# Selected rows of a routed layer processed one batch at a time

## The chip, the core and the metric

The kernel runs on one core of a Trainium2 chip. A core has five engines that work side by side, each through its own instructions in order: TensorE (PE, matrix products and transposes), VectorE (DVE), ScalarE (ACT), GpSimd (POOL) and SyncE (SP, which here only issues DMA transfers). They meet through semaphores. The metric is the time of one execution on the device, in microseconds (us); less is better.

## The reference

Two sequences (batches) of 2048 rows of 512 numbers go through four parts, each added to the rows with a gate:

```python
x = x + tanh(g_xattn[0]) * L0_xattn(layernorm(x), ctx)   # 16 heads over 128 context rows
x = x + tanh(g_ffn[0])   * L0_ffn(layernorm(x))          # routed, see below
x = x + tanh(g_xattn[1]) * L1_xattn(layernorm(x), ctx)   # 16 heads of 64
x = x + tanh(g_ffn[1])   * L1_ffn(layernorm(x))          # ternary weights, a convolution
```

The second part is the one that the change concerns. It sends only 256 of the 2048 rows of each batch through a small layer, and leaves the others as they are:

```python
_, idx = top_k(x @ w_router, 256)
x_sel = x[idx]                                # per batch
h = rmsnorm(x_sel, g1)
q, k, v = split(h @ W_qkv.T)                  # 16 heads of 32
o = softmax(causal(q @ k.T / sqrt(32))) @ v
x_attn = o @ W_out.T
h2 = rmsnorm(x_sel + x_attn, g2)
x_ff = silu(h2 @ W1.T) * (h2 @ W2.T) @ W3.T   # 1365 hidden columns
out = x.at[idx].set(x_sel + x_attn + x_ff)
```

Nothing in it mixes the two batches.

## The kernel before

A row tile is 128 rows of 512 numbers; a block is four row tiles (512 rows), so there are eight blocks, four for each batch. The stages follow each other in the program text; a scheduler then orders the instructions of each engine, mostly by their place in the text and by when their inputs and buffers are ready, and adds the semaphore waits.

**First cross attention, with the router beside it.** `cross_attention` runs 16 units per block (`U`), each one head: scores (L271), softmax (L116 to L128), transposes (L289), values (L297). `front` normalizes and transposes a block's rows, `back` multiplies with the output weights (L315) and updates the residual rows `x` (L324). All 32 row tiles of `x` stay in SBUF from the start (`load_x`, L430). When a block's rows are done, `router` (L442) is appended to `pending`; its steps are taken by `beside`, two after every unit. A router step normalizes rows again, writes them to `xn_d`, scores them (L462), writes the scaled residual to `x_d` (L473), and then counts on DVE for every row how many rows of its batch score higher (`count`, L492, and L514 for the 128 rows of the own tile). After the last block of a batch, `gather` makes one-hot matrices of the ranks (L537), multiplies them into the row numbers `idx` (L541, L555), and POOL fetches the 256 chosen rows into `xs` with an indirect DMA (L557). The router of the very last block has no units left to stand beside: it is drained by the loop at L589.

**Selected attention.** Both batches' 512 chosen rows are treated as one block (L644 to L785). `rms_block` normalizes and transposes them (L626), L674 makes values, `queries_keys` (L692) queries and keys of four heads at a time for both batches, 512 columns wide. `selected_probabilities` takes one batch: scores (L711), mask and maximum on DVE (L721, L722), exponentials on ACT (L727), a product with the reciprocal on POOL (L737). `selected_values` transposes (L747), copies (L748) and multiplies with the values (L752); it is called one step behind, so that one batch's softmax stands beside the other's products. L775 is the output projection; a second `rms_block` makes `h2T`.

**Feed-forward.** 1365 hidden columns in 11 chunks of 128 (`NF`). A chunk loads three slices of weights (`load_ffn`, three chunks ahead), multiplies two of them with `h2T`, 512 columns wide (L875), applies Silu (L883) and a product (L885), and accumulates the third (L861) into four PSUM tiles. Beside it, `quantized_weights` reads the two weight matrices of the last part, sums their absolute values (L819), and makes them ternary (L836 on ACT, L841 and L842 on DVE). At the end POOL adds the result into `x_d` with an indirect DMA (L902), four times.

**Second cross attention.** `W1.keys_values()` (L912) makes keys (L182) and values (L200) of the context; then `cross_attention` runs again, with rows from `x_d` (`xf`, L1143), residual rows read a second time, a bias added to them on POOL (L311), and the last part beside it.

Of the kernel before, what the change touches and what calls it, by code (L numbers as in the profile page):

```python
# [17 lines left out]
P = 128  # L18
# [3 lines left out]
BLK = 512  # L22
# [21 lines left out]
def flamingo_kernel(ctx: ExitStack, tc: tile.TileContext, a: dict, out: bass.AP):  # L44
# [91 lines left out]
    class CrossWeights:  # L136
# [38 lines left out]
        def keys_values(self):  # L175
            L, nE, bias = self.L, self.nE, self.bias
            with ExitStack() as st:
                ps0 = psum_pool(st, L + "ps0", 2)
                for e in range(nE):
                    pk = ps0.tile([P, B * M], F32, name="pk", tag="pk")  # L180
                    for c in range(CC):
                        nc.tensor.matmul(  # L182
                            pk,
                            self.wk[:, c, ts(e, P)],
                            self.ctxT[:, c, :],
                            start=(c == 0),
                            stop=(c == CC - 1),
                        )
                    src = pk.rearrange("p (b m) -> p b m", b=B)
                    if bias:  # L190
                        nc.vector.tensor_scalar(
                            self.kT[:, :, e, :], src, self.bk[:, e : e + 1], None, ALU.add
                        )
                    else:
                        nc.vector.tensor_copy(self.kT[:, :, e, :], src)
                for b in range(B):
                    for n in range(nE * P // 512):
                        pv = ps0.tile([P, 512], F32, name="pv", tag="pv")
                        for c in range(CC):
                            nc.tensor.matmul(  # L200
                                pv,
                                self.ctxT[:, c, ts(b, M)],
                                self.wv[:, c, ts(n, 512)],
                                start=(c == 0),
                                stop=(c == CC - 1),
                            )
                        to = self.v[:, b, ts(n, 512)]
                        if bias:
                            nc.vector.tensor_tensor(to, pv, self.bv[:, ts(n, 512)], ALU.add)
                        else:  # L210
                            nc.scalar.copy(to, pv)
# [159 lines left out]
    sel_stack = ExitStack()  # L371
# [19 lines left out]

    with ExitStack() as st:
        xres = st.enter_context(tc.tile_pool(name="xres", bufs=1))
        x = [xres.tile([P, D], F32, name=f"x{i}") for i in range(NT)]
        rp = st.enter_context(tc.tile_pool(name="router", bufs=1))
# [34 lines left out]
        def load_x(i):  # L430
            for t in range(i * TB, (i + 1) * TB):
                nc.sync.dma_start(out=x[t], in_=x_in[t])

        pending = []
# [7 lines left out]
        def router(n, tiles):  # L442
# [13 lines left out]
            for i in range(TB):  # L456
                t = t0 + i
                xn = act.tile([P, D], F32, name="xn2", tag="xn2", bufs=2)
                normalize(xn, x[t], mv, rstd, i)
                nc.sync.dma_start(out=xn_d[b][ts(t - b * TPB, P), :], in_=xn)  # L460
                ws = act.tile([P, D], F32, name="ws2", tag="ws2", bufs=1)
# [21 lines left out]
        def ranks(b, blk):  # L483
# [6 lines left out]
            def count(t, lo, hi, op, k):  # L490
                junk = rp.tile([P, S], BF16, name="junk", tag="junk", bufs=2)
                nc.vector.tensor_scalar(  # L492
                    junk[:, lo:hi], sb[b][:, lo:hi], own(t), None, op, ALU.add,
                    accum_out=cnt[b][:, t, k : k + 1],
                )
# [71 lines left out]
        with ExitStack() as st0:  # L567
            W0.load_context(st0, "left")
            load_x(0)
            W0.load_rest()  # L570
            for i in range(1, B * NBLK):
                load_x(i)
            W0.keys_values()
        act = st.enter_context(tc.tile_pool(name="L0_act", bufs=2))
        row = st.enter_context(tc.tile_pool(name="L0_row", bufs=8))
        ps_mm = psum_pool(st, "L0_mm", 2)
        ps_sc = psum_pool(st, "L0_sc", 4)
        ps_o = psum_pool(st, "L0_o", 2)

        def stage1_rows(n):  # L580
            tiles = x[n * TB : (n + 1) * TB]
# [7 lines left out]
        while pending:  # L589
            beside(None)  # L590


    right, right1, right2 = ExitStack(), ExitStack(), ExitStack()
# [3 lines left out]
    with ExitStack() as st:  # L597
        AHEAD = 3
        wst = st.enter_context(tc.tile_pool(name="wst", bufs=AHEAD))
        keepp = st.enter_context(tc.tile_pool(name="keepp", bufs=1))  # L600
        w13 = {}

        def load_ffn(f):
            n = min(P, DFF - f * P)
            w1c = wst.tile([P, DC, P], F32, name="w1c", tag="w1c")
            nc.sync.dma_start(
                out=w1c[:, :, :n], in_=row_tiles(a["W1T"])[:, :, ds(f * P, n)]
            )
            w2c = wst.tile([P, DC, P], F32, name="w2c", tag="w2c")
            nc.sync.dma_start(  # L610
                out=w2c[:, :, :n], in_=row_tiles(a["W2T"])[:, :, ds(f * P, n)]
            )
            w3c = wst.tile([P, D], F32, name="w3c", tag="w3c")
            nc.sync.dma_start(out=w3c[:n, :], in_=a["W3T"][ds(f * P, n), :])
            w13[f] = (w1c, w2c, w3c)

        g1 = keepp.tile([P, DC], F32, name="g1")
        nc.sync.dma_start(out=g1, in_=a["g1"])
        g2 = keepp.tile([P, DC], F32, name="g2")
        nc.sync.dma_start(out=g2, in_=a["g2"])  # L620
        xa = [keepp.tile([P, D], F32, name=f"xa{i}") for i in range(4)]

        def wide(name):
            return keepp.tile([P, DC, BLK], F32, name=name, tag="wide", bufs=2)

        def rms_block(tiles, gcol, dst, pool, ps, tag, name):  # L626

            ss = pool.tile([P, 4], F32, name=name + "_ss", tag="rms_ss")
            hn = [pool.tile([P, D], F32, name="hn", tag="hn", bufs=4) for _ in tiles]
            for i, t in enumerate(tiles):  # L630
                nc.scalar.activation(hn[i], t, AF.Square, accum_out=ss[:, i : i + 1])
            r = rsqrt(4, ss, 1.0 / D, 1e-6, small, name + "_r")
            for i, t in enumerate(tiles):
                nc.vector.tensor_scalar(hn[i], t, r[:, i : i + 1], None, ALU.mult)
            transpose_block(
                ps,
                tag,
                hn,
                lambda d, pt: nc.vector.tensor_scalar(
                    dst[:, d, :], pt, gcol[:, d : d + 1], None, ALU.mult  # L640
                ),
            )

        with ExitStack() as sa:  # L644
            w = sa.enter_context(tc.tile_pool(name="w_attn", bufs=1))
            act = sa.enter_context(tc.tile_pool(name="act_attn", bufs=1))
            row = sa.enter_context(tc.tile_pool(name="row_attn", bufs=6))
            ps_mm = psum_pool(sa, "s2_mm", 2)
            ps_sc = psum_pool(sa, "s2_sc", 4)
            ps_tp = psum_pool(sa, "s2_tp", 2)  # L650

            wqkv = w.tile([P, DC, 3 * D], F32, name="wqkv")
            for n in range(3):
                nc.sync.dma_start(
                    out=wqkv[:, :, ts(n, D)], in_=row_tiles(a["WqkvT"])[:, :, ts(n, D)]
                )
            wout = w.tile([P, DC, D], F32, name="wout")
            nc.sync.dma_start(out=wout, in_=row_tiles(a["WoutT"]))
            for f in range(AHEAD):
                load_ffn(f)  # L660

            mask = w.tile([P, 3, P], F32, name="mask")
            nc.gpsimd.memset(mask[:, 1, :], 0.0)
            for k in (0, 2):
                make_causal_mask(nc, mask[:, k, :], NEG)

            hT = wide("hT")
            rms_block(xs, g1, hT, act, ps_tp, "tp", "rms1")

            v2 = act.tile([P, 4, D], F32, name="v2")  # L670
            for i in range(4):
                pv = ps_mm.tile([P, D], F32, name="pv2", tag="mm")
                for d in range(DC):
                    nc.tensor.matmul(  # L674
                        pv,
                        hT[:, d, ts(i, P)],
                        wqkv[:, d, ds(2 * D, D)],
# [3 lines left out]
                nc.scalar.copy(v2[:, i, :], pv)  # L681

            OT = wide("OT2")

            def queries_keys(c):

                qc = act.tile([P, BLK], F32, name="qc", tag="qc", bufs=2)
                kc = act.tile([P, BLK], F32, name="kc", tag="kc", bufs=2)
                pq, pk = [ps_mm.tile([P, BLK], F32, name=n, tag="mm") for n in ("pq2", "pk2")]
# [73 lines left out]
            for c in range(DC):  # L763
                qc, kc = queries_keys(c)
                for b in range(B):
                    A = selected_probabilities(qc, kc, b)
                    if behind:
                        selected_values(*behind)
# [590 lines left out]
```

## Time and profile before

| | us |
|---|---|
| median of five runs | 1854.13 (1853.56 to 1855.94) |
| the profiled execution | 1853.55 |
| its span, first to last instruction | 1851.8 |
| PE busy in the span | 1658.2 (90%) |
| DVE busy | 1311.9 (71%) |
| ACT busy | 1051.4 (57%) |
| POOL busy | 526.5 (28%) |

The page gives busy time of each engine, the same in 40 slices of the span, the chain of work that ended last, and groups of equal instructions with their mean duration and the idle time ahead of them. An engine's busy share is a mean over stages; what one stage costs is read from its own stretch. The granted clock of PE is a share of its full speed; its mean here is 0.952. The first cross attention ends at 531.6 us of the span, the second begins at 835.0.

### The profile page before, as it was taken

Reading aid. Unit: us, or ns where it says so; the run is one execution under the profiler, and the core shown is the slowest. Engines: PE = TensorE matmul, PEld = TensorE weight load, DVE = VectorE, ACT = ScalarE, POOL = GpSimd, SP = SyncE. Lnnn points to the kernel's source line nnn. Section 1 sums busy time; section 2 is a strip of 40 time slices with the busy share of each in tenths; the row PEclk is TensorE's granted clock in tenths of the full one; section 3 lists DMA queues with packets and bytes.
Section 4 is the critical chain, followed back from the end, with each engine's and each line's share of the span. In section 5 each row is a group of like instructions: output and inputs, shape, how many; then the busy total and the mean of one; then the engine's idle time right before and its main releaser. Section 6 shows DMA issues by size and latency. Waiting matters only on the chain.

```text
span 1851.8 us, 24500 instructions
## 1 busy us (share of the span) xinstructions
PE 1658.2 (90%) x7706; PEld 832.6 (45%) x7706; DVE 1311.9 (71%) x2769; ACT 1051.4 (57%) x3065; POOL 526.5 (28%) x666
## 2 busy tenths in 40 slices
PE   6989988888836989989999999999999999898969
PEld 3544544444413444445544454444444454443423
DVE  5777898787783642224537789889888888876966
ACT  2645545354501536304537778878787787754556
POOL 4534434342300320032214233332423243220200
PEclk9999999899967889999999999999999999998989
DMA  7011011011144009330011233334134133255465
GB/s 287 1 46 47 1 47 46 12 46 47 46 141 154 1 11 313 111 91 23 29 37 50 97 114 105 128 118 155 52 130 129 73 116 120 77 203 202 152 226 194
DMA packets 98456, 184.36 MB, mean 100 GB/s; under 512 B 11327, under 2 KB 30527, under 8 KB 94614
## 3 DMA queue, kind: packets, MB, share of 16 engines
q1 hardware_dynamic: 97430, 180.70, 28.1%
q0 software_dynamic: 896, 2.10, 0.6%
q8 instruction: 61, 1.00, 0.2%
q14 instruction: 69, 0.57, 0.1%
HBM read 108.31 MB, written 74.45 MB: 99 GB/s over the span
## 4 chain that ended last, share of the span: by engine, by line
PE 38%; DVE 13%; DMA 5%; ACT 4%; POOL 2%; issue 2%; SPq 1%; POOLq 0%; DVEq 0%; ACTq 0%
PE pp L315 9%; PE pq L248 8%; PE ph L1002 3%; DVE h L1018 3%; PE sc L271 3%; PE po L297 2%; PE pu L875 2%; PE tp L289 2%; PE acc L861 2%; PE pw L875 2%; PE po L1231 2%; DMA hq<-hq_d 1%; DMA x<-h_d 1%; DVE u L1012 1%; DVE AT L290 1%
## 5 line engine op out<-in xcount | busy, mean ns | idle before, releaser
L119 ACT ACTIVATE A<-sc,nmx 128x128 f32<-128x128 f32 x1024 | 362.8, 376 | 174.4 <-DVE nmx L116 152.1
L128 POOL TENSOR_TENSOR A<-A,rden 128x512 f32<-128x512 f32 x256 | 274.7, 1074 | 479.6 <-DVE rden L127 368.4
L315 PE MATMUL pp<-L_wo,OT 128*128 128x512 f32 x768 | 365.9, 610 | 13.8 <-DVE x L324 4.7
L248 PE MATMUL pq<-xnT,L_wq 128*128 128x512 f32 x768 | 355.6, 609 | 0.0
L119 ACT ACTIVATION_READ_ACCUMULATOR A<-sc,nmx 128x1 f32 x1024 | 220.7, 216 | 0.0
L116 DVE TENSOR_REDUCE nmx<-sc 128x4 f32<-128x512 f32 x256 | 169.3, 678 | 66.4 <-PE sc L271 66.4
L248 PEld LDWEIGHTS pq<-xnT,L_wq 128*128 128x128 f32 x768 | 144.9, 196 | 158.5 <-issue 150.9
L290 DVE COPY AT<-tp 128x512 f32<-128x512 f32 x256 | 173.2, 678 | 56.0 <-PE tp L289 55.5
L315 PEld LDWEIGHTS pp<-L_wo,OT 128*128 128x128 f32 x768 | 138.7, 195 | 160.4 <-issue 134.3
L1018 DVE SCALAR_TENSOR_TENSOR h<-u,cw,h 128x512 f32<-128x512 f32 x256 | 191.6, 784 | 5.8 <-ACT h L1014 5.4
L289 PE MATMUL tp<-ident,A 128*128 128x128 f32 x1024 | 164.1, 282 | 30.0 <-POOL A L128 28.4
L271 PE MATMUL sc<-L_kT,qT 32*128 32x128 f32 (+1 forms) x2048 | 164.7, 292 | 6.6 <-ACT A L119 4.9
L271 PEld LDWEIGHTS sc<-L_kT,qT 32*128 32x128 f32 (+1 forms) x2048 | 131.2, 190 | 85.9 <-issue 59.7
L289 PEld LDWEIGHTS tp<-ident,A 128*128 128x128 f32 x1024 | 119.3, 143 | 105.1 <-issue 47.6
L1231 PE MATMUL po<-w2q,hq 128*128 128x512 bf16 x512 | 120.6, 391 | 18.1 <-DVE hq L1213 8.5
L1014 ACT ACTIVATE h<-u,cb,cw 128x512 f32<-128x512 f32 x128 | 99.1, 809 | 64.6 <-DVE u L1012 59.9
L1002 PE MATMUL ph<-xiT,w1q 128*128 128x512 bf16 x512 | 125.2, 381 | 2.6 <-DVE u L1012 2.4
L297 PE MATMUL po<-AT,L_v 128*32 128x512 f32 (+1 forms) x512 | 116.0, 625 | 8.0 <-DVE AT L290 7.6
L305 ACT COPY OT<-po 128x512 f32<-128x512 f32 x96 | 55.7, 588 | 101.2 <-PE po L297 100.8
L1012 DVE TENSOR_TENSOR u<-ph,inv_b 128x512 f32<-128x512 f32 x128 | 85.2, 684 | 31.0 <-PE ph L1002 26.1
L1011 POOL COPY u<-carry 128x2 f32<-128x2 f32 x128 | 49.7, 390 | 193.6 <-DVE h L1018 161.3
L311 POOL TENSOR_TENSOR x<-x,L_bo 128x512 f32<-128x512 f32 x64 | 86.8, 1374 | 34.2 <-DMA x<-x_d 8.2
(216 smaller groups left out, 2203.6 us busy)
## 6 DMA issues: line engine op xcount, KB each, us to landing
h_d<-h SPq DMA_DIRECT2D x28, 1024.0 KB, 3.9
x_d<-x SPq DMA_DIRECT2D x64, 256.0 KB, 2.6
hf<-h_d SPq DMA_DIRECT2D x64, 256.0 KB, 3.2
x<-x_d SPq DMA_DIRECT2D x61, 256.0 KB, 4.2
x<-h_d SPq DMA_DIRECT2D x48, 256.0 KB, 5.5
x<-in_x SPq DMA_DIRECT2D x32, 256.0 KB, 5.4
xn_d<-xn SPq DMA_DIRECT2D x32, 256.0 KB
xf<-x_d SPq DMA_DIRECT2D x32, 256.0 KB, 4.1
```

The lines of the kernel that those rows point to most:

```text
L116: nc.vector.tensor_reduce(nmx, sc, AX.X, ALU.max, negate=True)
L119: nc.scalar.activation(out_tile[:, h, :], sc[:, h, :], AF.Exp, bias=nmx[:, h : h + 1], accum_out=den[:, h : h + 1],)
L128: nc.gpsimd.tensor_tensor(out_tile, out_tile, rden.unsqueeze(2).to_broadcast([P, n, width]), ALU.mult,)
L248: nc.tensor.matmul(pq, W.wq[:, d, ts(e, P)], xnT[:, d, :], start=(d == 0), stop=(d == DC - 1),)
L271: nc.tensor.matmul(sc[h][:, t, :], qT[e % cpg][r, ts(t, P)], W.kT[r, b, e, :], start=True, stop=True,)
L289: nc.tensor.transpose(tp[:, t, :], A[:, t, :], ident)
L290: nc.vector.tensor_copy(AT, tp.rearrange("p t n -> p (t n)"))
L297: nc.tensor.matmul(po[h * dh : (h + 1) * dh, :], W.v[:, b, ts(hd, dh)], AT[c * hpc + h], start=True, stop=True,)
L315: nc.tensor.matmul(pp, OT[e][:, ts(i, P)], W.wo[:, e, :], start=(e == 0), stop=(e == nE - 1),)
L1002: nc.tensor.matmul(ph, w1q[:, d, ts(c, P)], xiT[g][:, d, :], start=(d == 0), stop=(d == DC - 1),)
L1018: nc.vector.scalar_tensor_tensor(z, u[:, ds(k, BLK)], cw[:, c, k : k + 1], z, ALU.mult, ALU.add)
L1231: nc.tensor.matmul(po, rows(c), w2q[:, c, :], start=(c == 0), stop=(c == HC - 1))
```

## The change

The selected rows are no longer one block of 512 but two of 256, each with its own attention and its own feed-forward.

- `selected_attention(b, ...)` is a generator: it yields after every small step. The first batch's is driven after the cross attention, with two calls of `beside` (each up to two router steps) after each of its own steps, and so stands beside the last block's router. The second batch's is handed to the feed-forward of the first, which takes five of its steps after every chunk, and two of the ternary weights' steps.
- `feed_forward(b, ...)` runs twice, 256 columns wide, with two accumulators; each run loads all weights of the layer. Beside the second run stand the keys and values of the next cross attention, of which `keys_values` is now a generator too. Each run scatters its own two row tiles into `x_d`.
- The residual rows are a ring of twelve row tiles: `load_x(n)` is called from `stage1_rows`, and a tile's buffer is free again when its scaled row is written to `x_d`.
- The weights `wqkv` are loaded at the start of the kernel, and `w1q` lies in the pool `const`.
- PSUM: while the feed-forward of the first batch runs, three banks are shared by its products, the queries, keys and values, two serve the scores, one the transposes and the products with the values, two accumulate.

```diff
-        x = [xres.tile([P, D], F32, name=f"x{i}") for i in range(NT)]
+    xres = router_stack.enter_context(tc.tile_pool(name="xres", bufs=3 * TB, side="right"))
...
+        def load_x(n):
+            if n * TB not in x:
+                for t in range(n * TB, (n + 1) * TB):
+                    x[t] = xres.tile([P, D], F32, name="x", tag="x")
+                    nc.sync.dma_start(out=x[t], in_=x_in[t])
...
-                junk = rp.tile([P, S], BF16, name="junk", tag="junk", bufs=2)
+                junk = rp.tile([P, S], BF16, name="junk", tag="junk", bufs=1)
...
-            for i in range(1, B * NBLK):
-                load_x(i)
-            W0.keys_values()
+            for n in (1, 2):
+                load_x(n)
+            for n in range(3):
+                nc.sync.dma_start(
+                    out=wqkv[:, :, ts(n, D)], in_=row_tiles(a["WqkvT"])[:, :, ts(n, D)]
+                )
+            with ExitStack() as st1:
+                for _ in W0.keys_values(psum_pool(st1, "L0_ps0", 2), "kv"):
+                    pass
...
         def stage1_rows(n):
-            tiles = x[n * TB : (n + 1) * TB]
+            load_x(n)
+            tiles = [x[t] for t in range(n * TB, (n + 1) * TB)]
...
-        while pending:
-            beside(None)
...
+    def selected_attention(b, mm, sc_tile, o_tile, together):
+        rows = xs[2 * b : 2 * b + 2]
+        hT = keepp.tile([P, DC, CAP], F32, name="hT", tag="hT", bufs=1)
+        yield from rms_rows(rows, g1, hT, mm)
...
+        qk, behind = (yield from queries_keys(0)), None
+        for c in range(DC):
+            A = yield from probabilities(*qk)
+            if c + 1 < DC:
+                qk = yield from queries_keys(c + 1)
+            if behind:
+                yield from values(*behind)
+            behind = A, c
+        yield from values(*behind)
...
+        yield from rms_rows(rows, g2, h2T[b], mm)
...
+    with ExitStack() as sp:
+        ps_mm = psum_pool(sp, "s2_mm", 2)
+        ps_sc = psum_pool(sp, "s2_sc", 4)
+        first = selected_attention(
+            0, in_pool(ps_mm, "mm"), in_pool(ps_sc, "sc"), in_pool(ps_o, "o"), 4
+        )
+        for _ in first:
+            for _ in range(2):
+                beside(None)
+        while pending:
+            beside(None)
...
+            for f in range(NF):
+                n = min(P, DFF - f * P)
+                pu, pw = mm([P, CAP], "pu"), mm([P, CAP], "pw")
...
+                if f > 0:
+                    down(f - 1)
+                    if f - 1 + AHEAD < NF:
+                        load(f - 1 + AHEAD)
+                after_chunk(f)
+                for w, n in work:
+                    for _ in range(n):
+                        next(w, None)
...
+    with ExitStack() as sp:
+        mm = in_pool(psum_pool(sp, "s2b_mm", 3), "mm")
+        ps_sc = psum_pool(sp, "s2b_sc", 2)
+        ps_tp = psum_pool(sp, "s2b_o", 1)
+        second = selected_attention(1, mm, in_pool(ps_sc, "sc"), in_pool(ps_tp, "o"), 2)
+        feed_forward(
+            0,
+            psum_pool(sp, "s2b_acc", 1),
+            mm,
+            [(lambda st: second, 5), (lambda st: quantized_weights(st, mm), 2)],
+        )
...
+    with ExitStack() as sp:
+        mm = in_pool(psum_pool(sp, "s2c_mm", 3), "mm")
+        ps_kv = psum_pool(sp, "s2c_kv", 3)
+        feed_forward(
+            1,
+            psum_pool(sp, "s2c_acc", 1),
+            mm,
+            [(lambda st: W1.keys_values(ps_kv, "kv"), 2)],
+            lambda f: W1.load_rest() if f == 1 else None,
+        )
...
-    W1.keys_values()
```

The products, the softmax and the ternary weights are computed as before, on half as many columns at a time. Of the selected attention's small operations one is new in count: the minimum of two maxima is taken per head (four on 128x1) and not once for four heads.

## The prediction, made before the changed kernel was run

> **What bounds the kernel now.** I read the page's slices first, to see where TensorE (PE) is not full and its clock falls; then the busy times of four stretches in the middle; then PE and VectorE (DVE) in order of time; last the instruction groups, for durations.
>
> ```profile
> PE   6989988888836989989999999999999999898969
> ...
> PEclk9999999899967889999999999999999999998989
> ```
>
> A slice is 46.3 us. PE is the full engine nearly everywhere; the one deep hole is slice 12 (509 to 556 us), and the clock is lowest around it. The stretches:
>
> ```profile
> core 0: us, PE busy (x) PEld busy (x) DVE busy (x) ACT busy (x) POOL busy (x), PEclk, DMA share, GB/s
> 531.64:575.87 44.23, 5.27 (x37) 2.85 (x37) 31.13 (x96) 6.51 (x13) 5.04 (x9) 0.52 0.81 275
> 575.87:688.83 112.96, 102.52 (x573) 52.31 (x573) 56.04 (x119) 46.87 (x164) 25.35 (x25) 0.91 0.04 14
> 688.83:805.45 116.62, 116.62 (x274) 51.47 (x274) 29.69 (x59) 42.83 (x60) 0.87 (x1) 0.98 0.53 172
> 805.45:835.02 29.57, 20.82 (x74) 13.52 (x72) 9.66 (x24) 2.34 (x4) 16.96 (x18) 0.92 0.59 143
> ```
>
> They are the last block's router, the selected attention of both batches, the feed-forward, and the keys and values of the next cross attention with the wait behind them: 303.4 us from the last residual update (531.64) to the next stage's first transpose (835.02). In the first, PE works 5.3 of 44.2 us while DVE ranks. That hole is what the change aims at.
>
> ```profile
> 521.02 9.83 PE L315 MATMUL pp<-L_wo,OT 128*128 128x512 f32 x16 [4.74 <-DVE x L324]
> ...
> 560.27 4.15 PE L541 MATMUL pi<-place,oh 128*128 128x2 bf16 x32 [20.61 <-DVE oh L537]
> 575.87 1.46 PE L110 MATMUL ptr<-ident,hn 128*128 128x128 f32 x5 [11.45 <-DVE hn L634]
> ```
>
> After 4.74 us of idleness the 16 matmuls of L315 take 9.83 us, where 16 later ones take 6.9: idle PE also loses clock.
>
> **What stays.** From the first transpose of the next stage on, the 4,227 PE instructions stand in the same order in both built programs. So the change is worth what it moves that transpose (835.02) plus what it leaves undone there. PE's arithmetic in the middle is the same too, if 256-wide matmuls cost half of 512-wide ones:
>
> ```profile
> 805.45 10.53 PE L182 MATMUL pk<-L_ctxT,L_wk 128*128 128x256 f32 x48
> 815.81 10.46 PE L200 MATMUL pv<-L_wv,L_ctxT 128*128 128x512 f32 x24
> 835.02 1.34 PE L110 MATMUL ptr<-ident,xf 128*128 128x128 f32 x5 [8.75 <-issue]
> ```
>
> 10.36 us (to the next start) over 48 is 0.216 us, and 10.46 over 24 is 0.43: half, with weight loads hidden (each f32 matmul is two such instructions). Splitting the feed-forward by batch doubles its weight loads and its weight traffic, and costs PE nothing.
>
> **Residual ring and early load: 0.** A block's x loads now wait for the x_d writes three blocks before. On SP's queue the loads of block 3 stand right behind block 0's writes, some 13 units ahead of their use; a unit is 3.8 us (eight blocks in 491 us, 16 units each), so 50 us of other work hide 2.6 us of write and 5.4 us of load. Without that cover five blocks would lose 8 us each. The QKV weights (3.1 MB) now load at the start, where five x blocks (5.2 MB) no longer do.
>
> **A: first batch's attention beside the last router.** The built order puts the first two residual updates of the last block ahead of a 1408-wide count; so the 4.74 us wait and the slow clock after it mostly go. The two together are worth at most 4.7 + 2.9; I take 4.6: the last update at 527.0. From there, on DVE:
> - to the first count: 8.7 us now (540.31), plus 2 x 0.48 and 4 x 0.42 of the new rows' normalizing, plus four value matmul pairs that stand on PE ahead of the last score broadcast (4 x 0.86, 4.6 at a partly halved clock): 15.9.
> - to the index: 24.7 now (540.31 to 565.05), plus one chunk's four heads, each 0.55 mask, 0.54 maximum, 0.16 minimum, and three evictions of 0.42: 31.0.
> - three more chunks, each 5.0 for the heads, 2 x 0.69 copies, 0.42 and 0.2: 21.0, and 1.5 each for hand-offs between engines: 25.5.
> - the tail: last exponentials 1.3, reciprocal 0.2, three POOL products 3.1, transpose, copy, product and copy 1.9, two output matmuls 1.7, then 7.2 as now from the residual copy (681.61) to the first feed-forward matmul (688.83): 15.4.
>
> Sum 87.8. The second gather (5 us to land) lies under these chunks; its two issues (2.0 us on POOL) stand among the first chunk's products, whose transposes wait no longer for it than for the scores of the next chunk. Bounds: 79 without hand-offs and value wait; 102 if PE (46 of attention, 5 of router) ran at half clock throughout. The feed-forward then starts at 614.8 with one batch attended; it now starts at 688.83 with both.
>
> ```profile
> L836 ACT ACTIVATE wq<-wr,wscale 128x1024 f32<-128x1024 f32 x16 | 17.4, 1140 | 11.2 <-DVE wscale L831 8.2 <-DVE w2b L841 3.0
> L737 POOL TENSOR_TENSOR A<-A,rden 128x512 f32<-128x512 f32 x24 | 24.3, 1042 | 71.9 <-DVE rden L735 71.9
> L721 DVE TENSOR_TENSOR A<-sc,mask 128x384 f32<-128x384 f32 x32 | 16.6, 550 | 6.1 <-PE sc L711 5.2 <-PE tp L747 0.9
> L748 DVE COPY AT<-tp 128x512 f32<-128x512 f32 x16 | 11.0, 687 | 18.0 <-PE tp L747 17.9
> L883 ACT ACT_TABLE_LOAD x1 | 1.3, 1283 | 11.7 <-issue 11.7
> ```
>
> (Columns: busy us, mean ns | idle before, releasers.)
>
> **B: first feed-forward with the second attention and the ternary weights.** PE: 11 chunks of 16 x 0.216 and 4 x 0.43, 56.9; attention: values 6.9, queries and keys 13.8, scores 4.4, 12 groups of transposes 6.6, products 4.0, output 6.9, row transposes 3.2, together 45.8: 102.7. New waits: the transposes have one PSUM bank instead of two, so each group waits for the copy before it, and in the built DVE order a ternary pair (0.69 and 0.43) often stands ahead; eight such copies at 1.5 are 12; the second pair of heads waits for mask adds, 8 x 0.5: 16 in all. B is 119. From below 103; from above 138, in the second rival. ACT gets ten more table loads (62 in the built program against 52), since exponentials and Silu now alternate: 12.8 us on an engine with some 62 of other work in 119 (ternary 16 x 1.14, sums 9.9, half of the exponentials 20.3, copies and Silu some 13).
>
> The row L883 shows 1.28 us for a table load, and nothing idle behind it. The Trainium skill, "ScalarE: Activation LUTs", section "What ACT_TABLE_LOAD costs", adds a drain of about 1.38 us to each switch and advises finishing one set first; that speaks against this change. By it, an estimate, the ten cost 26.6 us of ACT, and B would be up to 14 us longer if all of it delayed PE; no such drain shows here, so I go by the row.
>
> **C: second feed-forward with keys and values: 78.6.** The chunks' 56.9, the key and value products' 10.4 and 10.5, which only change their place, and 0.8 of hand-off. Below 77.6; above 86 if the first weights come late: some 17 MB are to be read, 54 us at the 313 GB/s of slice 16.
>
> **The next stage's start: +2.3.** Its first x rows no longer wait for the last scatter, since batch 0's is done early: the 8.75 us of "issue" idleness goes. What is late next: the eight residual adds of POOL (L311, 9.94 us, now beside the key products) come behind the scatter of batch 1 and, on POOL, ahead of the first normalization. That is then ready at 1.5 + 7 (two of four scatters that take 12.7) + 2.6 + 9.9 + 2.1 = 23.1 us; its transposes come 20.8 us into the stage now (855.79). Bounds 0 and 6.
>
> **Sum.** 527.0 + 87.8 + 119 + 78.6 + 2.3 = 814.7 against 835.0: 20.3 us less. Span 1851.8 becomes 1831.5; the profiled execution took 1853.55, 1.75 beyond its span, and the median 0.6 more: **1834 us**. Start, A, B, C and head each off by a third of their bounds give 1822 to 1847.
>
> **Rivals.**
> - *Hand-offs vanish:* A at 80, B at 108. For it: PE's queue has feed-forward matmuls between most attention steps. Against: attention alone ran at 102.5 busy of 113. 1834 - 8 - 11 = 1815.
> - *ACT and DVE become the bound in B (slower):* every one of the 12 transposes waits behind one ternary step (1.14 on ACT, 0.69 and 0.43 on DVE), 27 us instead of 12, and the 12.8 of table loads fall on PE as well: B is 147, time 1862. Decides from B = 139. For it: two in-order engines now serve three streams. Against: ACT has 75 of work in 119, DVE some 57 (heads 20, ternary 18, copies 5.5, the rest 13).
> - *No hiding:* the router finishes first and the batch follows alone, 44.2 + 65 in place of 87.8: 1855. The built order speaks against it: attention stands between the counts on DVE.
> - *Clock:* A at its upper bound and B 6 longer, by gaps like the one at 560: 1854.
>
> **Chances.** Forecast 0.60, hand-offs vanish 0.17, slower B 0.13, no hiding 0.05, clock 0.05. A measurement here tells 0.2% (3.7 us). Faster 0.77; within 0.2% 0.07 (the clock case and part of no hiding); slower 0.16. The range reaches down past 1815 and up to where a slower B begins: 1812 to 1858.
>
> **What would show it.** First feed-forward matmul (`pu`) at 610 to 620; the second half's at 728 to 740; first `xf` transpose near 812 with no idle time before it; 256-wide matmuls every 0.216 us; table loads of 1.28 us on ACT with PE not waiting for them. I am wrong if PE idles more than 35 us in B, if A takes over 100, or if the next stage starts with a POOL wait over 6 us.

## The result, and the profile after

The changed kernel takes 1858.21 us (median of 35 runs, 1852.1 to 1864.5), the kernel before beside it 1854.72 (60 runs, 1848.42 to 1863.06): ratio 1.0016, 95% interval 1.0009 to 1.0024. The forecast was 1834, with 1812 to 1858 as range. The profiled execution took 1858.27 us, its span is 1856.4, and the clock's mean is 0.952 as before.

First the page's slices of the changed kernel, then four stretches of it: the first batch's attention beside the router, the two feed-forwards, and the head of the next stage.

```profile
PE   6998888788877899998999999999999999898969
...
PEclk9999999899987899998999999999999999998989
```

```profile
core 0: us, PE busy (x) PEld busy (x) DVE busy (x) ACT busy (x) POOL busy (x), PEclk, DMA share, GB/s
539.95:627.96 88.01, 64.26 (x357) 39.29 (x357) 63.10 (x174) 38.18 (x112) 17.24 (x19) 0.78 0.34 117
627.96:751.72 123.76, 116.71 (x545) 79.29 (x546) 58.11 (x133) 66.72 (x138) 15.96 (x14) 0.92 0.54 173
751.72:829.25 77.53, 77.53 (x293) 54.85 (x292) 16.00 (x38) 6.57 (x15) 4.27 (x3) 1.00 0.43 117
829.25:873.04 43.79, 36.89 (x146) 21.25 (x144) 16.40 (x33) 15.53 (x59) 21.21 (x22) 0.81 0.29 84
```

The deep hole of slice 12 is filled (7 where there was a 3), and yet nothing is won. The landmarks say where it went. All are starts of instructions, so the forecast's 527.0, an end, stands here as 526.3; "head" is from the next stage's first transpose to its first transpose of softmax weights, "+16" from there to the 17th such transpose.

| us | before | forecast | after |
|---|---|---|---|
| last residual update | 530.9 | 526.3 | 539.2 |
| to first feed-forward product (A) | | 88.5 | 88.8 |
| first feed-forward (B) | | 119 | 123.8 |
| second feed-forward (C) | | 78.6 | 77.5 |
| next stage's first transpose | 835.0 | 812.4 | 829.2 |
| head | 20.7 | 23.1 | 26.4 |
| +16 | 12.4 | 12.4 | 17.3 |
| span | 1851.8 | 1831.5 | 1856.4 |

A and C are right, B is 4.8 too short. But the stretch starts 12.9 us later than forecast, and the next stage loses 8.2 more within its first 44 us.

**Where the start went.** Per block, the last residual update of the changed kernel lies within 3.2 us of the one before up to block 3 (299.6 and 296.4; blocks count from 0), and 9.7 behind at block 4 (384.0 and 374.3). VectorE (DVE) in order of time there, then TensorE (PE), then the queue of SyncE (SP):

```profile
354.45 0.35 DVE L545 TENSOR_SCALAR oh<-iota_r,rank 128x256 bf16<-128x256 f32 x1 [0.51 <-PE pi L549]
...
357.82 0.69 DVE L96 BATCH_NORM_STATS2 L_ln_st<-x 128x6 f32<-128x512 f32 x1
...
361.63 1.25 DVE L96 BATCH_NORM_STATS2 L_ln_st<-x 128x6 f32<-128x512 f32 x2
...
367.27 3.81 DVE L101 TENSOR_SCALAR xn<-x,L_ln_mv,L_ln_rstd 128x512 f32<-128x512 f32 x4 [0.57 <-POOL L_ln_rstd L87]
```

```profile
367.88 1.15 PE L110 MATMUL ptr<-ident,xn 128*128 128x128 f32 x4 [1.79 <-DVE xn L101]
369.74 0.69 PE L110 MATMUL ptr<-ident,xn 128*128 128x128 f32 x2 [0.71 <-DVE xn L101]
371.14 0.69 PE L110 MATMUL ptr<-ident,xn 128*128 128x128 f32 x2 [0.72 <-DVE xn L101]
```

```profile
308.45 0.92 SPq L481 DMA_DIRECT2D x_d<-x  x2
309.46 2.68 SPq L442 DMA_DIRECT2D x<-in_x  x4
```

L96 takes the statistics of block 6. They come after the first batch's last one-hot (L545), and PE waits for the normalized rows (L101), 1.79 us and then between every pair. The rows themselves were there some 40 us earlier: SP issued their load at 309.46 (2.68 us of issues; a load of such rows lands in 3.4 us, the median of this kernel), behind the scaled rows of block 3 as the ring demands. In the kernel before all rows were resident, and the same statistics stood ahead of the one-hots:

```profile
280.71 0.67 DVE L96 BATCH_NORM_STATS2 L_ln_st<-x 128x6 f32<-128x512 f32 x1
```

So no transfer is late; the order on DVE is. Between 363 and 376 us PE waits 5.2 us in all; around the same transposes of the kernel before (358 to 371) it waits 1.5.

**Where the head went.** PE and GpSimd (POOL) at the next stage's start:

```profile
829.25 1.94 PE L110 MATMUL ptr<-ident,xf 128*128 128x128 f32 x16
...
849.60 2.07 PE L272 MATMUL sc<-L_kT,qT 64*128 64x128 f32 x14 [2.88 <-ACT A L119]
855.70 2.11 PE L290 MATMUL tp<-ident,A 128*128 128x128 f32 x8 [4.02 <-POOL A L128]
857.74 2.07 PE L272 MATMUL sc<-L_kT,qT 64*128 64x128 f32 x8
859.74 2.07 PE L249 MATMUL pq<-xnT,L_wq 128*128 128x512 f32 x2
```

```profile
830.10 1.61 POOL L869 DMA_INDIRECT x_d<-xa,idx  x1 [19.45 <-DVE xa L868]
836.62 1.55 POOL L869 DMA_INDIRECT x_d<-xa,idx  x1 [4.92 <-DMA xf<-x_d]
...
842.51 1.04 POOL L87 TENSOR_TENSOR L_ln_rstd<-L_ln_rstd_e,neghalf 128x4 f32<-128x4 f32 x1
844.32 10.32 POOL L312 TENSOR_TENSOR x<-x,L_bo 128x512 f32<-128x512 f32 x8 [0.77 <-DMA x<-x_d]
854.59 2.05 POOL L128 TENSOR_TENSOR A<-A,rden 128x512 f32<-128x512 f32 x2
```

The first transpose has no idle time before it, as forecast. Then POOL, in its order, issues both scatters of the second batch (12 us with the gap between them and behind), takes the reciprocal root of block 1 (L87), adds the bias to eight row tiles (10.32 us), and only then normalizes the first softmax (L128). PE waits 2.88 and 4.02 us. The first of these waits is put down to ACT, but it goes back to POOL too: ACT waits for maxima that stand on DVE behind the normalization of block 1, and that waits 5.11 us for its root on POOL. Afterwards eight products that take 1.16 us in the kernel before take 2.07. The kernel before, at the same place:

```profile
855.72 1.10 PE L289 MATMUL tp<-ident,A 128*128 128x128 f32 x8
856.75 1.16 PE L271 MATMUL sc<-L_kT,qT 64*128 64x128 f32 x8
```

### The profile page after: what moved, and what is told of

The parts are those of the page before. It is cut to its first block, busy times and chain, and to the rows that moved or that the text cites. A ratio compares the mean times of both kernels' runs of the same rounds, so it can differ in the third digit from the quotient of the medians.

```text
span 1856.4 us, 25157 instructions
## 1 busy us (share of the span) xinstructions
PE 1673.6 (90%) x7946; PEld 883.8 (48%) x7946; DVE 1328.6 (72%) x2818; ACT 1063.8 (57%) x3090; POOL 527.0 (28%) x668
## 4 chain that ended last, share of the span: by engine, by line
PE 28%; DVE 13%; DMA 6%; ACT 4%; POOL 2%; issue 1%; SPq 0%; POOLq 0%; DVEq 0%; ACTq 0%
PE pp L316 9%; PE pq L249 7%; PE ph L1051 3%; PE po L298 2%; PE sc L272 2%; DVE h L1067 2%; PE tp L290 2%; PE po L1280 2%; DMA x<-h_d 1%; DVE u L1061 1%; POOL x L312 1%; DVE AT L291 1%; DVE nmx L116 1%; DMA h_d<-h 1%; DMA out_x<-x 1%
## 5 line engine op out<-in xcount | busy, mean ns | idle before, releaser
L128 POOL TENSOR_TENSOR A<-A,rden 128x512 f32<-128x512 f32 x256 | 273.8, 1071 | 483.0 <-DVE rden L127 375.1
L316 PE MATMUL pp<-L_wo,OT 128*128 128x512 f32 x768 | 370.3, 616 | 13.1 <-DVE x L325 6.1
L272 PE MATMUL sc<-L_kT,qT 32*128 32x128 f32 (+1 forms) x2048 | 160.4, 293 | 10.6 <-ACT A L119 8.1
L298 PE MATMUL po<-AT,L_v 128*32 128x512 f32 (+1 forms) x512 | 114.6, 619 | 10.6 <-DVE AT L291 10.2
```

The costliest lines, as they stand in the source:

```text
L128: nc.gpsimd.tensor_tensor(out_tile, out_tile, rden.unsqueeze(2).to_broadcast([P, n, width]), ALU.mult,)
L272: nc.tensor.matmul(sc[h][:, t, :], qT[e % cpg][r, ts(t, P)], W.kT[r, b, e, :], start=True, stop=True,)
L298: nc.tensor.matmul(po[h * dh : (h + 1) * dh, :], W.v[:, b, ts(hd, dh)], AT[c * hpc + h], start=True, stop=True,)
L316: nc.tensor.matmul(pp, OT[e][:, ts(i, P)], W.wo[:, e, :], start=(e == 0), stop=(e == nE - 1),)
```

## Experiments

Ratios are to the kernel before, run beside each of them on the same chip; the changed kernel stands at 1.0016. Landmarks are from one profiled execution each. From the 17th transpose of the next stage on, the remaining time differs between the profiled executions by 7 us (981 to 988), and the first stage differs too: in the eight kernels with sixteen row tiles and one count buffer the last residual update lies between 529.2 and 533.3. So a small difference of whole times is read from medians and intervals alone.

**1. A ring of sixteen row tiles.**

```diff
-    xres = router_stack.enter_context(tc.tile_pool(name="xres", bufs=3 * TB, side="right"))
+    xres = router_stack.enter_context(tc.tile_pool(name="xres", bufs=4 * TB, side="right"))
...
-            for n in (1, 2):
+            for n in range(1, 4):
                 load_x(n)
```

> Ring of sixteen row tiles in place of twelve, nothing else. Theory (the ring holds the statistics back): with twelve tiles a block's rows are loaded behind the scaled rows of three blocks before, and its statistics, which stood one block earlier on DVE, now stand within the block before it; for the sixth block that is behind the ranks and one-hots of the first batch (its normalized rows were ready 10 us later). With sixteen tiles the statistics stand where they did: last residual update at 526 to 532 us (539.2 in the changed kernel), whole time 8 to 12 us less, 1846 to 1850. Rival (another part of the change costs the first stage its 8 us: the single buffer of the counts, the early load of the QKV weights, the attention between the last counts): last residual update at 536 to 542, time 1855 to 1861.

Measured: 1852.49 us, ratio 0.9969 (0.9956 to 0.9982); by the ratios 8.7 us less than the changed kernel, within the 8 to 12 expected (1852.49 itself lies above 1846 to 1850; the kernel before took 1858.66 on that chip); last residual update at 532.5, at the edge of 526 to 532. (The "sixth block" of the expectation is block 6.) DVE in order of time:

```profile
285.57 0.67 DVE L96 BATCH_NORM_STATS2 L_ln_st<-x 128x6 f32<-128x512 f32 x1
286.24 0.65 DVE L96 BATCH_NORM_STATS2 L_ln_st<-x 128x6 f32<-128x512 f32 x1
...
361.69 0.54 DVE L101 TENSOR_SCALAR xn<-x,L_ln_mv,L_ln_rstd 128x512 f32<-128x512 f32 x1
```

The statistics are back at 286. The first tile of block 6 is normalized at 306.56, the three others from 361.69 on; in the changed kernel the first comes at 367.27.

**2. The kernel before, with the ring of twelve alone** (rows loaded per block from `stage1_rows`, pool of `3 * TB`).

> The kernel before, with the ring of twelve row tiles alone. Theory (the ring holds the statistics back): the first stage ends 8 to 12 us later than in the kernel before, last residual update at 538 to 543 us, and nothing later makes it up: 1861 to 1866 us. Rival (the loss needs another part of the change): 1852 to 1857 us, last residual update at 529 to 533.

Measured: 1867.29 us, ratio 1.0057 (1.0038 to 1.0077), by the ratio 10.6 us more than the kernel before; last residual update at 539.5, 8.6 later. One part of the change, put into the old kernel, costs what the first stage lost. This settles the start.

**3. Residual rows of the next stage's first two blocks early**, alone and with sixteen row tiles: loaded, and their bias added, after the fifth chunk of the second feed-forward.

```diff
...
+        if f == 4:
+            for n in range(2):
+                early[n] = [xr.tile([P, D], F32, name="x3", tag="x3") for _ in range(TB)]
+                for i, t in enumerate(early[n]):
+                    nc.sync.dma_start(out=t, in_=x_d[0][ts(n * TB + i, P), :])
+                    nc.gpsimd.tensor_tensor(t, t, W1.bo, ALU.add)
...
```

> The residual rows of the next stage's first two blocks are loaded, and their bias added on POOL, beside the second feed-forward; all else as changed. Theory (the eight adds hold up POOL at the head): the first transposes of softmax weights come 20.5 to 22 us after the stage's first transposes (26.5 in the changed kernel, 20.7 before), with no wait for POOL over 1 us ahead of them, and the time falls by 5 to 10 us: 1848 to 1853. Rival (the head's loss is made up in later blocks anyway, where the lag fell from 5.9 to 2.9 us, or another wait takes its place): 1855 to 1859.

> Sixteen row tiles and the early residual rows together. Theory (two separate losses): the gains add, 13 to 22 us less than the changed kernel, 1836 to 1845, near the 1834 that was predicted. Rival (one loss hides the other, or the later stages give it back): not under 1847.

Measured: 1855.73, ratio 0.9986 (0.9971 to 1.0002), and with sixteen row tiles 1845.37, 0.9944 (0.9926 to 0.9962). By the ratios that is 5.6 us less alone, at the lower end (the median alone lies in the rival's 1855 to 1859), and 13.4 for both, near the sum of 8.7 and 5.6: two separate losses. Heads of 19.9 and 20.2 us replace 26.4, and C grows from 77.5 to some 79. But "+16" stays at 19.2 and 18.1, so of the rival "another wait takes its place" holds in part. PE, then DVE, of the second kernel:

```profile
842.23 1.16 PE L272 MATMUL sc<-L_kT,qT 64*128 64x128 f32 x14 [1.44 <-ACT A L119]
843.56 0.66 PE L290 MATMUL tp<-ident,A 128*128 128x128 f32 x4 [0.18 <-POOL A L128]
844.95 1.08 PE L290 MATMUL tp<-ident,A 128*128 128x128 f32 x4 [0.74 <-POOL A L128]
845.97 2.07 PE L272 MATMUL sc<-L_kT,qT 64*128 64x128 f32 x8
847.97 2.07 PE L249 MATMUL pq<-xnT,L_wq 128*128 128x512 f32 x2
```

```profile
838.12 1.91 DVE L101 TENSOR_SCALAR xf<-xf,L_ln_mv,L_ln_rstd 128x512 f32<-128x512 f32 x4 [5.11 <-POOL L_ln_rstd L87]
```

Three gaps of 2.4 us in all are followed by 7 us at half speed. Their cause is one engine further back: DVE waits 5.11 us for a root on POOL, which stands behind the scatters, and the maxima of the first softmax wait behind it on DVE.

**4. The statistics of those two blocks early as well** (`ln_stats` of the early rows, ahead of the adds).

> As the run with sixteen row tiles and early residual rows, and the statistics of the next stage's first two blocks are taken from those early rows too. Theory (a second queue behind the scatter): at the head, block 1's normalization on DVE waited 5.11 us for its reciprocal root on POOL, which stood behind the second batch's scatter; with it the first maxima were late, PE idled 1.4 us and then ran at half clock for 8 us. With the root taken early DVE has no wait for POOL over 1.5 us in the first 20 us of the stage, PE does not fall to half clock there, and the time is 4 to 6 us less than without: 1839 to 1842 beside the 1845 of that run. Rival (the slow clock there comes from something else): within 1.5 us of that run.

Measured: 1842.12, ratio 0.9924 (0.9900 to 0.9947). Head 18.1, "+16" 12.4, as in the kernel before. PE:

```profile
839.02 1.10 PE L292 MATMUL tp<-ident,A 128*128 128x128 f32 x8
840.04 1.16 PE L274 MATMUL sc<-L_kT,qT 64*128 64x128 f32 x8
841.13 1.12 PE L251 MATMUL pq<-xnT,L_wq 128*128 128x512 f32 x2
```

No wait, full speed. In time it is 3.7 us less than without, just under what was expected, and the intervals of the two overlap; the landmarks carry the verdict.

**5. Two buffers for the counts again** (`junk`, `bufs=2`).

> As the run with early statistics, with two buffers for the counts' unused output again instead of one. DVE's order in the first stage is then that of the kernel before. Theory (the single buffer spread the counts between the softmax steps and costs the 3 to 4 us that the first stage still lacks at its third block): the third block's last residual update at 232 to 234 us instead of 236, the eighth's at 527 to 529 instead of 532, time 3 to 4 us less than with one buffer. Rival (those microseconds differ from execution to execution): no difference over 1.5 us.

Measured: 1847.12, ratio 0.9944 (0.9923 to 0.9964). Blocks 2 and 6 end at 232.4 and 490.3, as in the kernel before to 0.1 us and some 3 us ahead of the run with one buffer. But the next experiment's kernel has the same order of PE and DVE in the first stage, and there they end at 235.7 and 493.7: these 3 us can lie between executions, as the rival has it, and that the single buffer delays the middle of the stage isn't shown. What holds in both is the last block: 40.5 us with two buffers instead of 37.7 with one. The single buffer spreads the counts, and that lets the last updates in. A is 92.2 here instead of 88.7, but 88.9 in the next kernel, which has no ternary steps there, so it isn't the buffer alone. In whole time the theory was wrong: by the ratios 3.7 us more, with intervals that overlap.

**6. The ternary weights beside the second feed-forward.**

> As the run with two count buffers, and the ternary weights stand beside the second feed-forward instead of the first. Theory (the forecast's B: 12 of its 16 us of waits come from ternary pairs standing ahead of the copies on DVE): the first feed-forward with the second attention takes 112 to 116 us instead of 124, the second feed-forward stays at 78 to 80, since ACT and DVE have little there; time 6 to 11 us less. Rival (the waits are hand-offs of the attention itself, and the clock falls with them): first feed-forward 121 to 125 us, time within 2 us or more, as the ternary steps now reach into the next stage's head.

Measured: 1848.67, ratio 0.9964 (0.9945 to 0.9982). (The edit also gives the ternary steps one temporary buffer instead of two.) B is 110.3, 13.3 less than with the ternary steps in it; the forecast had blamed them for 12. C is 93.7, 14.3 more. The waits of PE in C (us in total, times, longest):

```profile
PE wtot L906 <- ACT wq L901: 6.9, 1, 6.9
```

The sum over partitions stands in PE's queue while the weights' rows are still being read, at 304 to 324 GB/s; ACT, which adds them up, waits up to 10.5 us for a transfer there. That much of the 14.3 goes back to the transfers.

**7. Two banks for the transposes, two instead of three for the products.**

> As the run with early statistics, and two PSUM banks for the second batch's transposes and value products, two instead of three for the shared products. Theory (the single bank makes each transpose group wait for the copy before it): the first feed-forward with the second attention takes 4 to 8 us less than 124. Rival (the third shared bank is worth as much, the feed-forward products then wait for Silu): 0 to 6 us more.

Measured: 1841.41, ratio 0.9915 (0.9890 to 0.9941); B 126.5, 2.8 more; in whole time no difference shows. For B the rival holds: the third bank for the products is worth at least as much as a second one for the transposes.

**8. One ternary matrix beside each feed-forward.**

> As the run with early statistics; the first ternary matrix stands beside the first feed-forward, the second beside the second, one step after each chunk instead of two, and the second one's sum over partitions on PE three chunks after its last partial sum. Theory (the ternary steps cost PE where they are dense: 13 us in the first feed-forward, and in the second, where all of them stood, 14, of which 6.9 were PE waiting for a sum whose rows came late at 304 to 324 GB/s): spread over both, the first feed-forward takes 115 to 118 us instead of 124 and the second 79 to 82, time 4 to 9 us less than the 1842 of that run. Rival (the second feed-forward is bound by its transfers, 20 MB in 79 us): what the first gains the second loses, within 2 us of that run.

Measured: 1842.64, ratio 0.9916 (0.9890 to 0.9942), no gain. B fell to 114.2, and the last product of the second feed-forward came 79.5 us after its first. But the next stage then waited:

```profile
PE ptr L110 <- DVE xf L101: 7.9, 2, 7.7
```

Its rows stood on SP behind the ternary matrix's writes. The head grew as well, to 21.5 us from 18.1.

**9. The first batch fetched last.** Two kernels: one moves the fetch in the text, behind the second batch's; the other adds a true dependence.

```diff
...
+            nc.vector.scalar_tensor_tensor(
+                chosen[0], row, 0.0, chosen[0], ALU.mult, ALU.add
+            )
+            nc.vector.tensor_copy(idx[:, 0:2], chosen[0])
...
```

> The changed kernel, with the first batch's rows fetched together with the second's, after the last one-hots, so that its attention can't stand beside the last router. Theory (the forecast's A: attention hidden beside the ranks): from the last residual update to the first feed-forward product 107 to 113 us instead of 88.8 (44 of router and 65 of attention), time 16 to 24 us more than the changed kernel, 1874 to 1882. Rival (attention beside the ranks runs at a low clock and hides little): 89 to 98 us, under 10 us more.

> The changed kernel, with the first batch's row numbers made to depend on the second's, so that its rows can't be fetched before the last one-hots (in the run that only moved it in the text, the built order put it back beside the counts). Theory (the forecast's A: attention hidden beside the ranks): from the last residual update to the first feed-forward product 105 to 113 us instead of 88.8, time 16 to 24 us more than the changed kernel. Rival (attention beside the ranks runs at a low clock and hides little): 89 to 98 us, under 10 us more.

Measured: the first 1861.06, ratio 1.0012 (0.9996 to 1.0027), A 88.7: it says nothing, since the scheduler put the attention back between the counts. The second 1881.51, ratio 1.0132 (1.0099 to 1.0164), A 110.6. Its waits of PE:

```profile
PE pi L550 <- DVE oh L546: 21.8, 1, 21.8
PE ptr L650 <- DVE hn L644: 17.9, 2, 14.2
```

PE waits for the ranks with nothing beside them. Hiding is worth 21.8 us of A; 44.2 + 65 - 87.8 of the forecast makes 21.4.

**10. Table loads.** Two kernels, both on the one with early statistics (B 123.7, with 11 table loads in it): in the first, the first feed-forward leaves the Silu out; in the second, the Silu is formed from a tanh.

```diff
-                nc.scalar.activation(su[:n, :], pu[:n, :], AF.Silu)
+                nc.scalar.activation(su[:n, :], pu[:n, :], AF.Tanh, scale=0.5)
+                nc.vector.scalar_tensor_tensor(
+                    su[:n, :], su[:n, :], 1.0, pu[:n, :], ALU.add, ALU.mult
+                )
...
-                nc.vector.tensor_tensor(gT[f][:n, :], pw[:n, :], su[:n, :], ALU.mult)
+                nc.vector.scalar_tensor_tensor(
+                    gT[f][:n, :], su[:n, :], 0.5, pw[:n, :], ALU.mult, ALU.mult
+                )
```

> As the run with early statistics; the first feed-forward leaves its Silu out and copies instead, so that ACT loads 52 tables in all instead of 62. Theory (a load costs 1.28 us of ACT and PE does not wait for most of them): the first feed-forward with the second attention takes 119 to 124 us, time 0 to 4 us less than the 1842 of that run. Rival (the switches are what slows it, as the note on table loads would have it): 108 to 114 us, 10 or more less.

> As the run with early statistics; Silu of u is formed as 0.5 u (1 + tanh(u/2)), the tanh on ACT and the two products on DVE, so that exponentials and the feed-forward share a table: 50 table loads instead of 62. Theory (the ten loads cost PE 8.3 us in the first feed-forward, as the run without Silu showed, 0.8 us each): first feed-forward 115 to 118 us instead of 123.7 and time 6 to 10 us less than the 1842 of the run with early statistics, 1832 to 1836. Rival (that gain came from leaving the Silu itself out; the 11 added DVE products, 0.45 us each, take it back): 121 to 124 us, time within 3 us.

Measured: without Silu 1827.05, ratio 0.9830 (0.9802 to 0.9857), B 115.4, between the two expectations. With tanh 1830.64, ratio 0.9852 (0.9825 to 0.9880), B 113.2, in spite of the added products on DVE. Neither has a table load left in B, so the 11 loads cost 8.3 and 10.5 us there. By the ratios the whole time fell by 17 and 13 us. The second agrees with its B within the intervals; half of the first isn't explained by its B (the profiled execution, 1835.03, was the slowest of its four). The version with tanh beats both kernels. Its first feed-forward (columns as above):

```profile
620.80:734.00 113.20, 110.38 (x545) 76.15 (x545) 61.66 (x145) 53.06 (x127) 15.28 (x14) 0.97 0.55 170
```

Beside the changed kernel's row: 6.3 us less of busy PE, a clock of 0.97 for 0.92, and 2.8 us idle where there were 7.0.

**11. Tanh, and one ternary matrix beside each feed-forward** (the second one's sum later, then two steps a chunk).

> As the run with tanh; the first ternary matrix beside the first feed-forward at one step a chunk, the second beside the second feed-forward, its sum over partitions after the fifth chunk and then two steps a chunk, so that its writes leave SP's queue before the next stage's rows are loaded. Theory (in the split run the first and second feed-forward together took 9.5 us less, 193.7 instead of 203, and 7.7 us were lost since the next stage's rows stood on SP behind the ternary writes): the two together 185 to 192 us, no wait over 2 us ahead of the stage's first transposes, time 4 to 9 us less than with tanh alone, 1825 to 1831. Rival (the second feed-forward has no room for the loads and the writes): within 2 us of the run with tanh.

Measured: 1832.69, ratio 0.9870 (0.9844 to 0.9895). B 112.7 and C 79.7 make 192.4, against 192.5 with tanh alone. The rival holds: once the loads are gone, moving the ternary steps wins nothing, and the head grew, to 22.7 us from 18.1.

## Why the prediction was wrong

- **Residual ring and early load: 0.** This step failed. It priced the ring as a transfer and asked what hides 2.6 us of write and 5.4 of load. That was answered rightly, no one waits for the load. What it didn't ask is where the instructions that read the rows now stand. The load's place moved the statistics by a block on DVE, for block 6 behind ranks and one-hots: 8.6 us of the first stage in the kernel before with the ring alone, 6.7 won back with four more row tiles (5.9 to 10.0 by the spread of the executions).
- **4.6 us from the last two updates.** Mis-sized: from block 6's last update to block 7's are 37.7 us now and 40.6 before, 2.9. The two kernels with two count buffers, where that block takes 40.5, show that the single buffer brings them, an edit that the sum didn't contain.
- **A, 87.8.** Right, 88.0 from the update's end, and for the reason given: 110.6 when nothing can stand beside the ranks. That it fits to 0.2 us is luck: the first count comes 15.0 us after the update (forecast 15.9), the index 29.3 after that (31.0), the feed-forward another 43.7 (40.9).
- **B, 119.** Measured 123.8, near in size and wrong in much of the mechanism. The ternary steps cost 13.3 us where 12 were put down to them, but not as eight waits of 1.5 us for the transposes' copies: PE waits for such a copy once for 2.7 us and once for 0.4. The longest:

```profile
PE tp L740 <- DVE AT L741: 2.7, 1, 2.7
```

A second bank for the transposes, paid for with one of the products', did not lower B. The table loads, costed at nothing for PE, take 8.3 to 10.5 us; this term failed as well. The two costs overlap: without the loads, moving half of the ternary steps wins 0.5, with them 9.5. The 16 us called waits are 7.0 of idle PE and some 14 of slower products, 116.71 busy for 102.7, at a clock of 0.92. Whether the ternary steps act through DVE or through ACT, where the loads stand too, isn't shown.
- **Table loads.** The Trainium skill, "ScalarE: Activation LUTs", section "What ACT_TABLE_LOAD costs", was weighed and set aside. The advice to do the calls of one set together stands in the same page's section "Table sets: the hidden batching unit", and here it was right. The size isn't this trace's: by an estimate from the page ten loads take 26.6 us of ACT, while here a load takes 1.28 us with 0.03 ahead of it and the next activation right behind, and B falls by 0.75 to 0.95 us for each of the 11 in it. The row L883 of the forecast shows idle time ahead of the load only; that none stands behind it is to be seen in a timeline. ScalarE (ACT) of the changed kernel:

```profile
692.82 1.28 ACT L849 ACT_TABLE_LOAD   x1
694.11 0.38 ACT L849 ACTIVATE su<-pu 128x256 f32<-128x256 f32 x1
694.52 1.28 ACT L720 ACT_TABLE_LOAD   x1
695.81 0.40 ACT L720 ACTIVATE A<-A,m 128x128 f32<-128x128 f32 x1
```

- **C, 78.6.** Right: 77.5, all of it busy. (Its lower bound of 77.6 should have been 77.8, the sum without the hand-off.)
- **The next stage's start, +2.3.** The eight adds of POOL were named, and their end was put at 23.1 us; it was 26.4, since the second scatter starts 4.92 us after the first has been issued and their rows are loaded behind both. The sum stopped at the first softmax. What it lacked is the root of block 1, on the same queue, and the slow products after the gaps: 4.9 us more in "+16", gone with the early statistics.
- **The stated signs of being wrong** all stayed silent: PE idles 7.0 us in B (limit 35), A takes 88.0 (100), and the stage's POOL wait is 4.02 us (6). None of them looked at the first stage or at the slow products. Of the signs of being right the three times failed, and named the place: first feed-forward product 628.0 (610 to 620), the second half's 751.7 (728 to 740), first transpose of the next stage 829.2 (812).
- **Added up:** start 12.9, A 0.2, B 4.8, C -1.1, next stage 9.4 (3.3 head, 4.9 in "+16", the rest within block 8, the next stage's first) make 26.2 us too little by block 8's end, of which 1.3 are made up later; 1831.5 + 24.9 is the span of 1856.4. The whole time lies near what three rivals give (1854, 1855 and 1862), but none of them holds: A is 88.0, B 123.8, and the attention is hidden. Of the rivals, the slower B had one right place and a cost of 4.8 where it needed 20. The right one, a lost lead on DVE in the stage before, was not on the list.

Left open: whether the 1 to 3 us of the first stage's blocks 2 and 3 belong to the change or lie between executions, and what makes the time after the head differ by 7 us between executions.

## What to carry to other kernels

- When a buffer becomes a ring, ask which instruction reads it, and where the scheduler now puts that instruction on its engine. Enough depth for the transfer isn't enough depth for the order; compare the built order of the readers, not only the queue of the loads.
- Work moved ahead of a stage's border uncovers what it used to hide. For each queue that crosses the border (here POOL: scatter, root, adds, first softmax) walk it to the second use, not to the first.
- Two streams with different activation tables on one engine paid for every change here, 0.75 to 0.95 us of PE's time each; a function that needed no change of table (tanh for Silu) removed it, at two products on DVE in place of one.

## Unexpected of the hardware

- After gaps of 1.4, 0.2 and 0.7 us PE ran at half speed for 7 us (products of 2.07 us for 1.16; granted clock 0.50 from 848 to 853 us, with sixteen row tiles and early residual rows). By an estimate, half of those 7 us, some 3.5 were lost after 2.4 of gaps; with the early statistics, which take the gaps away, the same products take 1.16 us.
- Of two scatters into the same tensor, POOL starts the second 4.92, 5.40 and 5.01 us after the first's issue (changed kernel, sixteen row tiles with early residual rows, early statistics); a scatter lands in 5.4. In the kernel before, where scatters into two tensors alternate, the gaps are 0.5 to 1.57 us. That the second waits for the first's landing fits, but the profile names another releaser each time, so it isn't shown.
